# Quarter products inside three of the seven block products of Q and K

## The chip, the cores and the metric

The kernel runs on one core of one Trainium2 chip. The metric is the device time of one execution in microseconds (us). The core has five engines that run side by side and wait for each other by semaphores: TensorE (PE; its weight loads are shown as PEld), VectorE (DVE), ScalarE (ACT), GpSimd (POOL) and SyncE (SP), which issues the transfers between HBM and the on-chip memory SBUF. Matrix products land in a third memory, PSUM, which here is held as four tiles of two banks each.

## The reference

Two layers of self-attention run one after the other on a batch of 8 images with 512 channels and 1024 positions, in float32. Cut to what matters:

```python
xn  = groupnorm(x) * gamma + beta                 # 8 groups in layer 0, 32 in layer 1
qkv = einsum('oc,bcn->bon', qkv_w, xn) + qkv_b    # 512 -> 3 x 512 channels
q, k, v = split(qkv)                              # 8 heads of 64 channels
attn = softmax(einsum('bhdi,bhdj->bhij', q, k) / 8)
out  = einsum('bhij,bhdj->bhdi', attn, v)
x    = einsum('oc,bcn->bon', proj_w, out) + proj_b + x
```

## The kernel before

A *unit* is one image in one layer; there are 16, numbered 0 to 15, and units 0 to 7 are layer 0. The main loop over `u` does, for each unit: Q, then K, then V (`projections`), then the output projection of the unit before (`project(old, ...)`), then `attention` of this unit. While attention runs, the next unit's input is normalised. The results of layer 0 go to HBM as `mid`. Every engine takes its instructions in the order in which the program writes them, and waits are set automatically between them from the tiles that they read and write.

**Seven block products.** `blocks` makes a 512 x 512 by 512 x 1024 product as two-by-two blocks with seven block products in place of eight (a fast matrix multiplication of the Strassen kind). The left factors, from the weights, are mixed once per layer (`mix_weights`), the right ones, from the activations, once per unit (`mix_right`). They are numbered 1 to 7 and used in the order 1, 6, 2, 7, 5, 4, 3. Three PSUM tiles gather the sums: `bx` (`apair[0]`), `by` (`sbank[0]`) and `bz` (`apair[1]`); the fourth, `sbank[1]`, is not used in this stage. A sum that is wanted more than once is copied or added into SBUF as `p1`, `u2`, `u3`. ScalarE's `c11` and VectorE's `others` write the four blocks of the result. `done` is called after each block product; it counts them as `g` and runs small jobs that were left for that place (`rest`): for example `g` = 10 is after K's third block product.

In Q and K one block product is four matmuls of 128 x 128 weights by 512 columns; in V, where the roles are exchanged, it is eight with 256 columns.

**Buffers that matter here.** The pool `ppool` has four buffers of 4 KB per partition. In attention they hold the exponentials `p`, between attentions the `u3` of Q, K and V and the four residual tiles `x` that `load_res` fetches. The `mid` stores (line 411) read the residual tiles, so the exponentials of the next attention get those buffers only when the stores are done. `vpool` has one buffer, V of the unit. `tpool` holds the mixed right factors, with the tags `x1`, `x2`, `x4` for the unit's input and `o1`, `o2`, `o4` for the attention output.

**SyncE's queue.** All transfers are issued by SyncE in program order: in a unit first the residual, then the next input (`load_xn`), in unit 7 the weights of layer 1 (`load_weights(1)`, which GpSimd then mixes), then the output projection's stores, then the small transfers of attention.

Of the kernel before, what the change touches and what calls it, by code (L numbers as in the profile page):

```python
# [11 lines left out]
F32 = mybir.dt.float32  # L12
# [6 lines left out]
P = 128  # L19
# [13 lines left out]
def fast_path(ctx, tc, x, qkv_wT, proj_wT, vecs, groups, out, flag):  # L33
# [14 lines left out]
    nc = tc.nc  # L48
    B, C, N = x.shape
    CC = C // P  # L50
    D = C // HEADS
    NT = N // P
    FD = 512
    NH = N // FD
    H = P // 2
    FD2 = FD // 2
    BL = 32
    SCALE = 1.0 / math.sqrt(D)
    assert D == H and C == FD

    def pool(name, bufs, **kw):
# [6 lines left out]
    vpool = pool("vpool", 1)  # L68
    qkpool = pool("qkpool", CC)
    ppool = pool("ppool", 4)  # L70
    accpool = pool("accpool", 2)
    tpool = pool("tpool", 1)
# [6 lines left out]
    mids = pool("mids", 1, space=bass.MemoryType.DRAM)  # L79


    sbank = [ps.tile([P, 2, FD], F32, tag=f"s{i}", name=f"s{i}") for i in range(2)]
# [8 lines left out]
    half = const.tile([P, CC], F32, name="half")  # L91
    okay = const.tile([P, 2 * BL], F32, name="okay")
    asum = const.tile([P, 2 * B * CC], F32, name="asum")
    mid = [mids.tile([C, N], F32, tag=f"mid{b}", name=f"mid{b}") for b in range(B)]

    units = [(l, b) for l in range(2) for b in range(B)]
# [54 lines left out]
    def mix_right(name, low, high):  # L151


        b11, b12 = low[:, :, :FD], low[:, :, FD:]
        b21, b22 = high[:, :, :FD], high[:, :, FD:]
        t1, t2, t4 = (
            tpool.tile([P, 2, FD], F32, tag=f"{name[0]}{k}", name=f"{name}_t{k}")
            for k in (1, 2, 4)
        )
        sub = nc.vector.tensor_sub  # L160
        parts = (
            partial(sub, t1, b12, b11), partial(sub, t2, b22, t1),
            partial(sub, t4, b21, t2), partial(sub, b12, b22, b12),
        )
        return {1: b11, 2: b21, 3: b22, 4: t4, 5: t1, 6: t2, 7: b12}, parts

    def load_proj(l, tag):
        w = wpool.tile([P, CC, C], F32, tag=tag, name=f"wproj_{l}_{tag}")
# [99 lines left out]
    class Unit:  # L268
        pass

    def blocks(name, left, right, tokens, c11, others, done, u3_in):

        bx, by, bz = apair[0], sbank[0], apair[1]
        sums = []

        def products(bank, k, start, stop):
            a, b = left[k], right[k]
            for i in range(4 if tokens else 2):  # L280
                if tokens:
                    dst = bank[:, i // 2, (i % 2) * FD2 : (i % 2 + 1) * FD2]
                else:
                    dst = bank[:, i, :]
                for c in range(2):
                    at, moving = (b, a) if tokens else (a, b)

                    nc.tensor.matmul(  # L288
                        dst, at[:, c, ts(i, P)], moving[:, c, :],
                        start=start and c == 0 and not (tokens and i % 2),  # L290
                        stop=stop and c == 1, skip_group_check=True,
                    )

        def work(pool, tag, k):
            sums.append(pool.tile([P, 2, FD], F32, tag=tag, name=f"{k}_{name}"))
            return sums[-1]

        products(bx, 1, True, False)
        p1 = work(accpool, "acc", "p1")
        nc.scalar.copy(p1, bx)  # L300
        done(sums)
        products(by, 6, True, False)
        u2 = work(trpool, "tr", "u2")
        nc.vector.tensor_add(u2, by, p1)  # L304
        done(sums)
        products(bx, 2, False, True)
        c11(bx)
        done(sums)
        products(by, 7, False, False)
        u3 = work(*u3_in, "u3")  # L310
        nc.vector.tensor_add(u3, by, p1)
        done(sums)
        products(bz, 5, True, False)
        others(1, 1, bz, u3)
        done(sums)
        products(by, 4, False, True)
        others(1, 0, by, p1)
        done(sums)
        products(bz, 3, False, True)
        others(0, 1, bz, u2)  # L320
        done(sums)

    def projections(w, rest):


        u = w.u
        l, _ = units[u]
        w.last = {"q": [], "k": [], "v": []}
        g = 0

        def done(_):
            nonlocal g
            g += 1
            for part in rest.get(g, ()):
                part()

        for sel, bias in (("q", QB), ("k", KB)):
            tiles = [
                qkpool.tile([P, N], F32, tag=sel, name=f"{sel}_{u}_{pr}") for pr in range(CC)
            ]  # L340

            def c11(bank):
                for i in range(2):
                    w.last[sel].append(
                        nc.scalar.activation(
                            tiles[i][:, :FD], bank[:, i, :], AF.Identity,
                            bias=vec[:, l, bias, i : i + 1],
                        )
                    )

            def others(r, h, bank, more):
                for i in range(2):
                    pr = 2 * r + i
                    w.last[sel].append(
                        nc.vector.scalar_tensor_tensor(
                            tiles[pr][:, ts(h, FD)], bank[:, i, :], vec[:, l, bias, pr : pr + 1],
                            more[:, i, :], ALU.add, ALU.add,
                        )
                    )

            left = w.lefts["qk".index(sel)]
            blocks(f"{sel}_{u}", left, w.right, False, c11, others, done, (ppool, "p"))
            setattr(w, sel, tiles)

        w.v = vpool.tile([P, NT, C], F32, tag="v", name=f"v_{u}")

        def of_tokens(t):
            return t.rearrange("p a (b o) -> p (a b) o", b=2)

        def v11(bank):  # L370
            w.last["v"].append(nc.scalar.copy(w.v[:, : NT // 2, :FD2], of_tokens(bank)))

        def v_others(r, h, bank, more):
            w.last["v"].append(
                nc.vector.tensor_add(  # L375
                    w.v[:, ts(h, NT // 2), ts(r, FD2)], of_tokens(bank), of_tokens(more)
                )
            )

        blocks(f"v_{u}", w.lefts[2], w.right, True, v11, v_others, done, (ppool, "p"))  # L380
# [72 lines left out]
            )  # L453
            nc.sync.dma_start(dst[o * P : (o + 1) * P, ts(h, FD)], cols)

    def attention(w, at_step):


        u = w.u
# [39 lines left out]
        def products(s):  # L499
            p = state["p"][s]  # L500
            c, t = divmod(s, NT)
            pr, qh = divmod(c, NH)
            banks = abank[2 * (c % 2) : 2 * (c % 2) + 2]
            before = [state["exp"][s]]
            if t == 0:
                before += state["free"][c % 2]
            if s == 0:
                before += w.last["v"] + w.evac_before
            gate(*before)
            for r in range(2):  # L510
                rows = slice(r * H, (r + 1) * H)
                for j in range(2):
                    lo = pr * P + j * D
                    nc.tensor.matmul(  # L514
                        banks[r][j * H : (j + 1) * H, :],
                        w.v[rows, t, lo : lo + D],
                        p[rows, j, :],
                        start=(t == 0),
                        stop=(t == NT - 1),
                    )  # L520
# [14 lines left out]
        def evacuate(c):  # L535
            pr, qh = divmod(c, NH)
            banks = abank[2 * (c % 2) : 2 * (c % 2) + 2]
            tmp = tmppool.tile([P, FD], F32, tag="tmp", name=f"tmp_{u}_{c}")
            i0 = nc.scalar.copy(tmp, banks[0])  # L539
            i1 = nc.vector.tensor_add(w.ao[pr // 2][:, pr % 2, ts(qh, FD)], banks[1], tmp)  # L540
            state["free"][c % 2] = [i0, i1]
# [71 lines left out]
        for s in range(n_steps):  # L613
            c, t = divmod(s, NT)
            p = scores(s)
# [13 lines left out]
            summed(s, p)  # L629
            at_step(s, state)  # L630
        products(n_steps - 1)
        evacuate(n_chunks - 1)

        for h in range(NH):
# [6 lines left out]
            for h in range(NH):  # L641
                add_bias(CC - 1, h)

        w.right_o, mixing = mix_right(f"o_{u}", *w.ao)
        return {4: [lambda: reciprocals(CC - 1)], 10: [divide_last], 12: mixing[:2], 14: mixing[2:]}


    xn = load_xn(0)
# [2 lines left out]
    lefts, mixing_w = mix_weights(0, load_weights(0), nc.vector)  # L651
# [11 lines left out]
    old = None  # L663
    for u in range(2 * B):
        w = Unit()
        w.u, w.right, w.lefts = u, right, lefts
        w.evac_before = []
        for part in mixing[2:]:
            part()
        if u == B + 1:  # L670
            rest[16] = mixing_o
        projections(w, rest)
# [12 lines left out]
        if u == B - 1:  # L685
            lefts, mixing_w = mix_weights(1, load_weights(1), nc.gpsimd)
            for part in mixing_w:
                part()

        def stats_of(*which):  # L690
            for i in which if nxt is not None else ():
# [36 lines left out]
            elif c == 2 + CC and t in (2, 5):  # L728
                mixing[int(t == 5)]()

        rest = attention(w, at_step)
        old = w

    both = const.tile([P, 1], F32, name="both")
# [275 lines left out]
```

## Time and profile before

| | |
|---|---|
| time, median of 3 runs | 3342.32 us (3341.9 to 3342.86) |
| span in the profile | 3340.0 us |
| TensorE busy | 3315.5 us, 99% |
| VectorE busy | 2375.6 us, 71% |
| ScalarE busy | 1393.5 us, 42% |
| GpSimd busy | 48.1 us, 1% |
| mean granted TensorE clock | 0.999 |
| from HBM / to HBM | 110.26 MB / 34.08 MB |

Busy time is the time in which an engine had an instruction in execution; the profile's other parts give the chain of waits that ended last, groups of like instructions with the idle time before them, and the transfers. Times within the execution count from the start of the span. A unit takes some 207 us: Q, K, V and the output projection 24 us each, the rest attention.

### The profile page before, as it was taken

Reading aid. Unit: us, or ns where it says so; the run is one execution under the profiler, and the core shown is the slowest. Engines: PE = TensorE matmul, PEld = TensorE weight load, DVE = VectorE, ACT = ScalarE, POOL = GpSimd, SP = SyncE. Lnnn points to the kernel's source line nnn. Section 1 sums busy time; section 2 is a strip of 40 time slices with the busy share of each in tenths; the row PEclk is TensorE's granted clock in tenths of the full one; section 3 lists DMA queues with packets and bytes.
Section 4 is the critical chain, followed back from the end, with each engine's and each line's share of the span. In section 5 each row is a group of like instructions: output and inputs, shape, how many; then the busy total and the mean of one; then the engine's idle time right before and its main releaser. Section 6 shows DMA issues by size and latency. Waiting matters only on the chain.

```text
span 3340.0 us, 51079 instructions
## 1 busy us (share of the span) xinstructions
PE 3315.5 (99%) x21002; PEld 1645.3 (49%) x21002; DVE 2375.6 (71%) x2977; ACT 1393.5 (42%) x1549; POOL 48.1 (1%) x32
## 2 busy tenths in 40 slices
PE   8999999999999999999999999999999999999999
PEld 4445454454544545455554544545445454454533
DVE  4876948769486684867848678585785957859577
ACT  1542706336063360733617235172451724517144
POOL 0000000000000000002000000000000000000000
PEclk9999999999999999999999999999999999999999
DMA  2011010110101102012020111201111011110121
GB/s 78 33 39 58 21 64 27 39 58 22 70 27 33 58 21 76 21 33 96 21 85 25 33 58 28 76 15 33 64 33 64 15 37 60 33 63 15 39 71 47
DMA packets 66844, 149.27 MB, mean 45 GB/s; under 512 B 20784, under 2 KB 21040, under 8 KB 66608
## 3 DMA queue, kind: packets, MB, share of 16 engines
q1 hardware_dynamic: 66608, 145.95, 13.3%
q8 instruction: 169, 2.77, 0.4%
q14 instruction: 67, 0.55, 0.1%
HBM read 110.26 MB, written 34.08 MB: 43 GB/s over the span
## 4 chain that ended last, share of the span: by engine, by line
PE 98%; DVE 1%; issue 0%; DMA 0%; ACT 0%; POOL 0%; SPq 0%; DVEq 0%
PE a L514 26%; PE a L288 26%; PE s L486 25%; PE s L288 19%; PE a L486 1%; PE s L437 0%; PE a L437 0%; DMA xn<-x_dram 0%; DVE acc L533 0%; DVE x L422 0%; DVE stats L184 0%; PE a L196 0%; DVE tr L546 0%; DVE u_o L390 0%; POOL y L216 0%
## 5 line engine op out<-in xcount | busy, mean ns | idle before, releaser
L494 ACT ACTIVATE p<-s 128x1024 f32<-128x1024 f32 x976 | 997.2, 1023 | 816.7 <-PE s L486 761.7
L514 PE MATMUL a<-p,v 64*64 64x512 f32 x8192 | 1101.2, 589 | 0.1
L486 PE MATMUL s<-q,k 64*64 64x512 f32 x7808 | 1059.3, 590 | 1.4 <-DVE v L375 1.4
L533 DVE TENSOR_TENSOR acc<-acc,p 128x1024 f32<-128x1024 f32 x768 | 938.7, 1222 | 88.8 <-ACT p L494 41.4
L514 PEld LDWEIGHTS a<-p,v 64*64 64x64 f32 x8192 | 384.9, 131 | 494.4 <-ACT p L494 349.6
L486 PEld LDWEIGHTS s<-q,k 64*64 64x64 f32 x7808 | 385.8, 133 | 437.1 <-issue 434.6
L288 PE MATMUL a<-xn,w 128*128 128x512 f32 x512 | 234.4, 601 | 4.0 <-DVE xn L244 4.0
L531 DVE TENSOR_TENSOR acc<-p,p 128x1024 f32<-128x1024 f32 x128 | 153.7, 1201 | 12.9 <-ACT p L494 12.9
L288 PEld LDWEIGHTS a<-xn,w 128*128 128x128 f32 x512 | 96.9, 192 | 132.7 <-issue 128.1
L546 DVE STREAM_TRANSPOSE tr<-acc 128x1024 f32<-128x1024 f32 x128 | 158.0, 1234 | 0.0
L556 DVE TENSOR_REDUCE red<-tr 128x32 f32<-128x1024 f32 x128 | 153.9, 1202 | 0.6
L540 DVE TENSOR_TENSOR ao<-a,tmp 128x512 f32<-128x512 f32 x128 | 88.0, 687 | 69.9 <-ACT tmp L539 69.9
L300 ACT COPY p_k<-a 128x1024 f32<-128x1024 f32 x16 | 16.2, 1012 | 255.1 <-PE a L288 255.1
L300 ACT COPY p_o<-a 128x1024 f32<-128x1024 f32 x15 | 15.2, 1012 | 244.2 <-PE a L288 244.2
L288 PE MATMUL a<-w,xn 128*128 128x256 f32 x512 | 115.7, 379 | 0.0
L288 PE MATMUL s<-xn,w 128*128 128x512 f32 x256 | 115.2, 593 | 0.4 <-DVE u_q L304 0.4
L300 ACT COPY p_v<-a 128x1024 f32<-128x1024 f32 x16 | 16.2, 1012 | 237.3 <-PE a L288 221.4
L288 PE MATMUL s<-x_t,s2w 128*128 128x512 f32 x256 | 115.1, 592 | 0.0
L288 PE MATMUL a<-x_t,s1w 128*128 128x512 f32 x256 | 115.1, 592 | 0.0
L288 PE MATMUL s<-x_t,w 128*128 128x512 f32 x256 | 115.1, 592 | 0.0
L288 PE MATMUL a<-xn,s4w 128*128 128x512 f32 x256 | 115.1, 592 | 0.0
L288 PE MATMUL a<-ao,wproj_wproj 128*128 128x512 f32 x240 | 107.9, 592 | 0.0
(129 smaller groups left out, 2843.4 us busy)
## 6 DMA issues: line engine op xcount, KB each, us to landing
rb<-drec SPq DMA_DIRECT2D x128, 256.0 KB, 3.9
xn<-mid SPq DMA_DIRECT2D x36, 512.0 KB, 5.0
xn<-x_dram SPq DMA_DIRECT2D x32, 512.0 KB, 5.1
x<-x_dram SPq DMA_DIRECT2D x32, 512.0 KB, 4.6
mid<-x SPq DMA_DIRECT2D x64, 256.0 KB, 2.1
x<-mid SPq DMA_DIRECT2D x28, 512.0 KB, 4.6
out_dram<-x SPq DMA_DIRECT2D x56, 256.0 KB, 2.1
w<-qkv_wT_dram SPq DMA_DIRECT2D x6, 1024.0 KB, 11.2
```

The lines of the kernel that those rows point to most:

```text
L288: nc.tensor.matmul(dst, at[:, c, ts(i, P)], moving[:, c, :], start=start and c == 0 and not (tokens and i % 2), stop=stop and c == 1, skip ...
L300: nc.scalar.copy(p1, bx)
L486: nc.tensor.matmul(bank[e * H : (e + 1) * H, j, :], w.k[pr][j * H : (j + 1) * H, t * P + e * H : t * P + (e + 1) * H], w.q[pr][j * H : (j ...
L494: exp = nc.scalar.activation(p, bank, AF.Exp, scale=SCALE)
L514: nc.tensor.matmul(banks[r][j * H : (j + 1) * H, :], w.v[rows, t, lo : lo + D], p[rows, j, :], start=(t == 0), stop=(t == NT - 1),)
L531: nc.vector.tensor_add(acc, state["first"], p)
L533: nc.vector.tensor_add(acc, acc, p)
L540: i1 = nc.vector.tensor_add(w.ao[pr // 2][:, pr % 2, ts(qh, FD)], banks[1], tmp)
L546: nc.vector.transpose(tr, state["acc"].pop(c))
L556: nc.vector.tensor_reduce(red[:, :, qh, :], state["tr"].rearrange("p j (f i) -> p j f i", i=BL), AX.X, ALU.add)
```

## The change

In units 1 to 15, three of the seven block products of Q and of K, those numbered 2, 3 and 4 (`INNER`), are themselves made by the same seven-product scheme, with quarter products of one 128 x 128 weight block by 256 columns. Of eight such quarters seven remain. They come in the order 1, 2, 3, 6, 5, 4, 7.

For this the quarter products need mixed factors of their own:

- The right factors are made in each unit by GpSimd, four additions of 128 x 256 for each of the three block products (`mix_inner`), into three buffers of `ppool`. The `u3` of Q and K, which lay there, moves into the end of the V buffer.
- The left factors are made once per layer by GpSimd (`mix_inner_left`, in units 0 and 7: 24 additions of 128 x 128), written to HBM by six transfers, and read back at the end of every attention into the V buffer, two loads of 1152 numbers per partition (`load_inner_left`).

Parts of the quarter products that can't be summed in the block product's own bank are gathered in free PSUM banks (`one`, `two`) and copied by ScalarE to an SBUF tile `rest`, four copies of 128 x 256 for each block product. `one` is copied out between its uses and goes on accumulating. Later GpSimd adds the parts of `rest` together and adds them to the tiles of Q or K (`add_rest`, `rests`): two additions of 128 x 256 and two of 128 x 512 for each block product. Since `rest` lies in the `o` buffers of `tpool`, mixing the right factors of the attention output moves from K's blocks (`g` = 12 and 14) to V's (17, 19 and 20).

```diff
+    def mix_inner(u, right):
+        gp = nc.gpsimd
+        factors, parts = {}, []
+        for k in INNER:
+            b = right[k]
+            b11, b12 = b[:, 0, :FD2], b[:, 0, FD2:]
+            b21, b22 = b[:, 1, :FD2], b[:, 1, FD2:]
+            t = ppool.tile([P, 4, FD2], F32, tag="p", name=f"r{k}_{u}")
+            t1, t2, t3, t4 = (t[:, i, :] for i in range(4))
+            parts += [
+                partial(gp.tensor_sub, t1, b12, b11), partial(gp.tensor_sub, t2, b22, t1),
+                partial(gp.tensor_sub, t3, b22, b12), partial(gp.tensor_sub, t4, b21, t2),
+            ]
+            factors[k] = {1: b11, 2: b21, 3: b22, 4: t4, 5: t1, 6: t2, 7: t3}
+        return factors, parts
...
+    def mix_inner_left(l, lefts):
+        add, sub = nc.gpsimd.tensor_add, nc.gpsimd.tensor_sub
+        for n, k in enumerate(INNER):
+            t = tpool.tile([P, 2, FD], F32, tag=("o1", "o2", "o4")[n], name=f"l{k}_{l}")
...
+            for i in range(2):
...
+                add(s1, a21, a22)
+                sub(s2, s1, a11)
+                sub(a21, a11, a21)
+                sub(s4, a12, s2)
+                nc.sync.dma_start(inner_left[l][:, i, n], t[:, i])
+
+    def load_inner_left(u):
+        l, _ = units[u]
+        flat = vpool.tile([P, NT, C], F32, tag="v", name=f"il_{u}").rearrange("p t o -> p (t o)")
...
+            nc.sync.dma_start(part, inner_left[l][:, i])
...
+        def last_products(bank, k, one, two):
...
+            rest = tpool.tile([P, 2, FD], F32, tag=tag, name=f"m{k}_{name}")
...
+            product(1, one, True, False)
+            nc.scalar.copy(rest[:, 0, :FD2], one)
+            product(2, bank[:, 0, :FD2], False, True)
+            product(3, bank[:, 0, FD2:], False, True)
+            product(6, one, False, False)
+            nc.scalar.copy(rest[:, 0, FD2:], one)
+            product(5, two, True, True)
+            nc.scalar.copy(rest[:, 1, FD2:], two)
+            product(4, bank[:, 1, :FD2], False, True)
+            product(7, one, False, True)
+            nc.scalar.copy(rest[:, 1, :FD2], one)
+            return rest
+
+        def add_rest(r, h, rest):
+            if rest is not None:
+                add = nc.gpsimd.tensor_add
+                add(rest[:, 0, FD2:], rest[:, 0, FD2:], rest[:, 1, FD2:])
+                add(rest[:, 1, FD2:], rest[:, 1, :FD2], rest[:, 1, FD2:])
+                rests(r, h, rest)
...
-        products(bx, 2, False, True)
+        rest = last_products(bx, 2, sbank[1], bz)
         c11(bx)
+        add_rest(0, 0, rest)
...
-        products(by, 4, False, True)
+        rest = last_products(by, 4, bx, sbank[1])
         others(1, 0, by, p1)
+        add_rest(1, 0, rest)
         done(sums)
-        products(bz, 3, False, True)
+        rest = last_products(bz, 3, sbank[1], bx)
         others(0, 1, bz, u2)
+        add_rest(0, 1, rest)
         done(sums)
...
+            def rests(r, h, rest):
+                for i in range(2):
+                    cols = tiles[2 * r + i][:, ts(h, FD)]
+                    w.last[sel].append(nc.gpsimd.tensor_add(cols, cols, rest[:, i, :]))
...
         products(n_steps - 1)
+        at_end()
         evacuate(n_chunks - 1)
...
-        return {4: [lambda: reciprocals(CC - 1)], 10: [divide_last], 12: mixing[:2], 14: mixing[2:]}
...
+            17: [partial(mix, 0, 1)], 19: [partial(mix, 2)], 20: [partial(mix, 3)],
...
+        if u > 0:
+            w.made = old.made_next
+            w.inner, parts = mix_inner(u, right)
+            for part in parts:
+                part()
...
+        if u in (0, B - 1):
+            mix_inner_left(units[u + 1][0], lefts)
...
+        def at_end():
+            if u + 1 < 2 * B:
+                w.made_next = load_inner_left(u + 1)
```

More of the change, by code (lines that the diff above doesn't have):

```diff
@@ L58, in fast_path @@
     SCALE = 1.0 / math.sqrt(D)
+    INNER = (2, 3, 4)
     assert D == H and C == FD
@@ L93, in fast_path @@
     asum = const.tile([P, 2 * B * CC], F32, name="asum")
+    inner_left = [
+        mids.tile([P, 2, len(INNER), 3, P], F32, tag=f"il{l}", name=f"il{l}") for l in range(2)
+    ]
     mid = [mids.tile([C, N], F32, tag=f"mid{b}", name=f"mid{b}") for b in range(B)]
@@ L165, in mix_right @@
         return {1: b11, 2: b21, 3: b22, 4: t4, 5: t1, 6: t2, 7: b12}, parts
+    def mix_inner(u, right):
[10 more added lines that the diff above has]
+                partial(gp.tensor_sub, t3, b22, b12), partial(gp.tensor_sub, t4, b21, t2),
+            ]
+            factors[k] = {1: b11, 2: b21, 3: b22, 4: t4, 5: t1, 6: t2, 7: t3}
+        return factors, parts
@@ new lines, in inner_lefts @@
+    def inner_lefts(k, left, made):
+        a11, a12 = left[:, 0, :P], left[:, 1, :P]
+        a21, a22 = left[:, 0, P:], left[:, 1, P:]
+        s1, s2, s4 = (made[:, i, :] for i in range(3))
+        return {1: a11, 2: a12, 3: s4, 4: a22, 5: s1, 6: s2, 7: a21}
+    def mix_inner_left(l, lefts):
+        add, sub = nc.gpsimd.tensor_add, nc.gpsimd.tensor_sub
+        for n, k in enumerate(INNER):
+            t = tpool.tile([P, 2, FD], F32, tag=("o1", "o2", "o4")[n], name=f"l{k}_{l}")
+            t = t.rearrange("p a b -> p (a b)")[:, : 6 * P].rearrange("p (i s o) -> p i s o", i=2, s=3)
+            for i in range(2):
+                left = lefts[i][k]
+                a11, a12 = left[:, 0, :P], left[:, 1, :P]
+                a21, a22 = left[:, 0, P:], left[:, 1, P:]
+                s1, s2, s4 = (t[:, i, j, :] for j in range(3))
+                add(s1, a21, a22)
[3 more added lines that the diff above has]
+                nc.sync.dma_start(inner_left[l][:, i, n], t[:, i])
@@ new lines, in load_inner_left @@
+    def load_inner_left(u):
+        l, _ = units[u]
+        flat = vpool.tile([P, NT, C], F32, tag="v", name=f"il_{u}").rearrange("p t o -> p (t o)")
+        n = len(INNER) * 3 * P
+        made = []
+        for i in range(2):
+            part = flat[:, i * n : (i + 1) * n].rearrange("p (k s o) -> p k s o", s=3, o=P)
+            nc.sync.dma_start(part, inner_left[l][:, i])
+            made.append({k: part[:, j] for j, k in enumerate(INNER)})
+        return made, flat[:, NT * C - 2 * FD :].rearrange("p (a b) -> p a b", a=2)
@@ L269, in fast_path, with blocks @@
         pass
-    def blocks(name, left, right, tokens, c11, others, done, u3_in):
+    def blocks(name, left, right, tokens, c11, others, done, u3, inner=None, rests=None):
         bx, by, bz = apair[0], sbank[0], apair[1]
@@ L292, in products, with product @@
                     )
+        def last_products(bank, k, one, two):
+            if inner is None:
+                products(bank, k, False, True)
+                return None
+            left, right = inner[k]
+            one, two = one[:, 0, :FD2], two[:, 0, :FD2]
+            tag = ("o1", "o2", "o4")[INNER.index(k)]
+            rest = tpool.tile([P, 2, FD], F32, tag=tag, name=f"m{k}_{name}")
+            def product(j, dst, start, stop):
+                nc.tensor.matmul(
+                    dst, left[j], right[j], start=start, stop=stop, skip_group_check=True
+                )
+            product(1, one, True, False)
[16 more added lines that the diff above has]
+                rests(r, h, rest)
         def work(pool, tag, k):
@@ L305, in blocks @@
         done(sums)
-        products(bx, 2, False, True)
+        rest = last_products(bx, 2, sbank[1], bz)
         c11(bx)
+        add_rest(0, 0, rest)
         done(sums)
         products(by, 7, False, False)
-        u3 = work(*u3_in, "u3")
+        if isinstance(u3, tuple):
+            u3 = work(*u3, "u3")
+        else:
+            sums.append(u3)
         nc.vector.tensor_add(u3, by, p1)
@@ L359, in others @@
                     )
-            left = w.lefts["qk".index(sel)]
-            blocks(f"{sel}_{u}", left, w.right, False, c11, others, done, (ppool, "p"))
+            def rests(r, h, rest):
+                for i in range(2):
+                    cols = tiles[2 * r + i][:, ts(h, FD)]
+                    w.last[sel].append(nc.gpsimd.tensor_add(cols, cols, rest[:, i, :]))
+            i = "qk".index(sel)
+            left, inner, u3 = w.lefts[i], None, (ppool, "p")
+            if w.inner:
+                made, u3 = w.made
+                inner = {
+                    k: (inner_lefts(k, left[k], made[i][k]), w.inner[k]) for k in INNER
+                }
+            blocks(f"{sel}_{u}", left, w.right, False, c11, others, done, u3, inner, rests)
             setattr(w, sel, tiles)
@@ L454, in project_last, with attention @@
             nc.sync.dma_start(dst[o * P : (o + 1) * P, ts(h, FD)], cols)
-    def attention(w, at_step):
+    def attention(w, at_step, at_end):
         u = w.u
@@ L642, in divide_last, with mix @@
                 add_bias(CC - 1, h)
-        w.right_o, mixing = mix_right(f"o_{u}", *w.ao)
-        return {4: [lambda: reciprocals(CC - 1)], 10: [divide_last], 12: mixing[:2], 14: mixing[2:]}
+        mixing = []
+        def mix(*which):
+            if not mixing:
+                w.right_o, parts = mix_right(f"o_{u}", *w.ao)
+                mixing.extend(parts)
+            for i in which:
+                mixing[i]()
+        return {
+            4: [lambda: reciprocals(CC - 1)], 10: [divide_last],
+            17: [partial(mix, 0, 1)], 19: [partial(mix, 2)], 20: [partial(mix, 3)],
+        }
     xn = load_xn(0)
@@ L665, in fast_path @@
         w = Unit()
-        w.u, w.right, w.lefts = u, right, lefts
+        w.u, w.right, w.lefts, w.inner = u, right, lefts, None
         w.evac_before = []
@@ L729, in at_step @@
                 mixing[int(t == 5)]()
-        rest = attention(w, at_step)
+        def at_end():
+            if u + 1 < 2 * B:
+                w.made_next = load_inner_left(u + 1)
+        rest = attention(w, at_step, at_end)
         old = w
```

## The prediction

> **What bounds the kernel now.** I read the page from the top: busy times, then the chain that ended last, then the costliest groups.
>
> ```profile
> PE 3315.5 (99%) x21002; PEld 1645.3 (49%) x21002; DVE 2375.6 (71%) x2977; ACT 1393.5 (42%) x1549; POOL 48.1 (1%) x32
> ...
> PE 98%; DVE 1%; issue 0%; DMA 0%; ACT 0%; POOL 0%; SPq 0%; DVEq 0%
> ...
> L539 ACT COPY tmp<-a 128x512 f32<-128x512 f32 x128 | 74.3, 581 | 23.9 <-PE a L514 23.9
> ...
> L300 ACT COPY p_k<-a 128x1024 f32<-128x1024 f32 x16 | 16.2, 1012 | 255.1 <-PE a L288 255.1
> ...
> x<-x_dram SPq DMA_DIRECT2D x32, 512.0 KB, 4.6
> ```
>
> TensorE is busy 99% and is 98% of the chain, so only a shorter matrix stream or new TensorE idling can move the time. GpSimd (POOL) is almost unused. The last three rows are prices used below: a ScalarE copy of 512 and of 1024 columns out of PSUM, and a 512 KB load.
>
> The timeline gives the pace of the matrix stream; columns are start, length, engine, line, operation, operands. These are products of Q (512 columns) at the start of unit 5:
>
> ```profile
> 1035.20 3.60 PE L288 MATMUL s<-x_t,s2w 128*128 128x512 f32 x8
> ...
> 1038.63 3.60 PE L288 MATMUL a<-xn,w 128*128 128x512 f32 x8
> ...
> 1042.06 3.60 PE L288 MATMUL s<-xn,w 128*128 128x512 f32 x8
> ...
> 1042.26 1.26 ACT L345 ACTIVATE q<-a,vec 128x512 f32<-128x512 f32 x2 [5.86 <-PE a L288]
> ```
>
> A block product takes 1038.63 - 1035.20 = 3.43 us for 8 records (each written float32 matmul shows as two), so 0.429 us a record. ScalarE starts reading 0.20 us after the next block's first start. In V the records have 256 columns:
>
> ```profile
> 1514.01 3.62 PE L288 MATMUL a<-s4w,xn 128*128 128x256 f32 x16
> ...
> 1517.47 3.60 PE L288 MATMUL a<-ao,wproj_wproj 128*128 128x512 f32 x8
> ```
>
> 16 of them take 3.46 us, or 0.215 each: half the columns cost half the time.
>
> Last, the hand-over to attention in unit 7, where the change puts one-time work:
>
> ```profile
> 1528.42 1.27 POOL L688 TENSOR_TENSOR s1w<-w 128x512 f32<-128x512 f32 x1 [165.85 <-DMA w<-qkv_wT_dram]
> ...
> 1528.75 15.47 SPq L411 DMA_DIRECT2D mid<-x  x8
> ...
> 1541.59 1.95 PE L486 MATMUL s<-q,k 64*64 64x512 f32 x16
> ...
> 1543.05 1.94 ACT L494 ACTIVATE p<-s 128x1024 f32<-128x1024 f32 x2 [20.90 <-DMA mid<-x]
> ...
> 1543.97 1.27 POOL L688 TENSOR_TENSOR s4w<-w,s2w 128x512 f32<-128x512 f32 x1
> ...
> 1544.90 1.07 PE L514 MATMUL a<-p,v 64*64 64x512 f32 x8
> ```
>
> The first exponential waits for a `mid<-x` store, because its output `p` takes the buffer of a residual tile that must first be stored. Even now the stores end just in time.
>
> **What the Trainium skill says.** "GPSIMD Engine Reference", section 3.1, gives 4497 ns for a GpSimd two-input add of 2048 float32. The trace shows 1.27 us for 512, and section 1's SBUF interface shared with VectorE fits the 1.71 us seen when VectorE is busy. "Perfetto Trace Analysis", section "DMA Instruction — HWDGE (DVE, Sync)", says that the issuing sequencer itself waits for a transfer's semaphore and is free only afterwards: one waiting transfer holds all behind it. Here SyncE does wait inside its queue for the `mid<-x` producers. "TensorE: Matmul & The Clock Gate", section "What's actually happening", has the clock fall to half in idle windows; the first 8 matmuls, after an idle start, agree:
>
> ```profile
> 16.96 6.32 PE L288 MATMUL a<-xn,w 128*128 128x512 f32 x8 [3.95 <-DVE xn L244]
> ```
>
> Their successor starts at 23.12, so they took 6.16 us and not 3.43: 2.7 us lost.
>
> **The change part by part.**
>
> *Removed.* In units 1 to 15, three block products of Q and three of K become 7 quarter products each, of two 256-column records: 14 x 0.215 = 3.01 us for 3.43. Saved: 0.43 us, times 6 x 15 = 90, is 38.6 us, all on TensorE and so on the path.
>
> *Added waits in the quarter products.* `one` and `two` are copied out by ScalarE before they are used again. Two quarter products (0.86 us) always lie between a product's end and the reuse. In that time: 0.20 us until ScalarE starts; the copy of 256 columns, by the line through 581 and 1012 ns, 0.37; the release; the weight load, 0.19 us in the trace. The release is read from attention:
>
> ```profile
> 1009.48 1.02 ACT L494 ACTIVATE p<-s 128x1024 f32<-128x1024 f32 x1
> ...
> 1010.62 0.49 PEld L514 LDWEIGHTS a<-p,v 64*64 64x64 f32 x8 [0.37 <-ACT p L494]
> ```
>
> It is 0.12 us. The sum 0.20 + 0.37 + 0.12 + 0.19 = 0.88 is 0.02 over 0.86. There are 8 such waits in Q, 8 in K (two in each block, one more where the next block takes `two` over), so 240: 4.6 us. Bounds: 0 if the load needn't wait, 0.12 each (29 us) if the whole hand-over is exposed. Behind the waiting matmul all of TensorE is queued. I take the sum, since each term is from a row.
>
> *GpSimd.* No row has 256 or 128 columns. Between proportional (0.64, 0.32) and the 512-column price (1.27) I take the line through the trace's 1.27 us and the skill's 4.5: 0.73 and 0.46, an estimate. The right factors are 12 x 0.73 = 8.8 us per unit. Their buffers come free in turn as the last `p` tiles are added up: four adds from 1025.86 to 1031.05 hold p_58 to p_61, so product 2's factors are ready near 1033, and its blocks come at 1038.6 (unit 5). Product 4's follow the VectorE mix ending at 1038.8: ready near 1043, wanted near 1048. The corrections are 6 x (2 x 0.73 + 2 x 1.27) = 24 us per unit; the last of K ends some 6 us into V, and attention waits for it only 48 us after K. So 33 us of GpSimd lie beside TensorE at no cost, twice as slow included except for product 4's factors.
>
> *Factors from HBM.* Two loads of 576 KB per unit leave when V's buffer is free, at the last attention product. With 4.6 us for 512 KB the first lands near +5.5 us; the third quarter product asks for it after two blocks and two quarters, 7.7 us. Hidden by 2 us; the second is for K, 24 us on.
>
> *Moved.* Mixing the attention output's right factors goes from K to V. VectorE has room there (the windows give it 8.6 us busy in unit 5's 24 us of V), and the output projection begins later: nothing. The extra copies, 24 x 0.37 = 9 us per unit, find ScalarE mostly idle in Q and K: no cost beyond the waits. VectorE's evacuations are as before.
>
> *One-time factors.* In unit 0 nothing waits behind them. In unit 7, 24 GpSimd adds follow the weight mixing that ends at 1545.24, and their six HBM writes stand in SyncE's queue ahead of unit 6's `mid<-x` stores. GpSimd ends at 1545.2 + 24 x 0.46 = 1556.3. Then the last write's issue (0.35), five stores at 0.46, and 2.1 us to land (page's median) free the first `p` buffer at 1561.0 in place of 1543.05: 17.9 us in which TensorE can only run three scores ahead. With the half clock after it, 2.7: 20.6 us. Bounds: 24 x 0.32 gives 17; 0.6 an add gives 24.
>
> Sum: 3342.3 - 38.6 + 4.6 + 20.6 = 3328.9, say 3329 us.
>
> **The rivals.**
> 1. The hold-up in unit 7 doesn't reach TensorE (other buffers free first, or stores pass). Against it: the 20.90 us wait on `mid<-x` shows the dependency. Time: 3342.3 - 38.6 + 4.6 = 3308.
> 2. Buffer reuse becomes the bound: 0.12 us at each of 240 waits. For it: my margin is 20 ns and the 256-column copy isn't in the trace. Against: V keeps 0.215 us a record with a weight load for each. 3342.3 - 38.6 + 20.6 + 29 = 3353, slower than before.
> 3. The HBM factors or GpSimd's right factors come 2 us late in every unit: 15 x 2 = 30 us, 3359. For it: both loads start at once and share the DMA engines. Against: by the windows the four 512 KB loads of `xn` issued from 1104.20 are all in by 1112, 2 MB in some 7 us.
>
> **How the numbers follow.** Forecast 0.45, rivals 0.27, 0.17, 0.11. The border of 0.2% lies at 3335.6 and 3349.0. Faster: 0.41 of the forecast, all of rival 1, 0.02 of rival 3's short delays: 0.70. Same: 0.04 + 0.05 + 0.04 = 0.13. Slower: 0.12 + 0.05 = 0.17. The range 3305 to 3353 runs from rival 1 to rival 2 and leaves out most of rival 3 and the ends of both.
>
> **What would show it.** Right: inner blocks of about 3.05 us with pauses of tens of ns before the reused quarter; POOL near 520 us (15 x 33 + 48) with the idle before it not on the chain; one TensorE gap of some 18 us at the start of unit 7's attention, with ScalarE waiting for `mid<-x`; the other units about 2.3 us shorter (38.6 less 4.6, over 15). Wrong: TensorE waits of 0.1 us or more on the new copies, waits on the factor load in each unit, or no gap in unit 7.

## The result and the profile after

| | before | after |
|---|---|---|
| time, median of 4 runs | 3342.17 us (3341.9 to 3342.86) | 3348.67 us (3348.15 to 3349.08) |
| ratio after / before | | 1.0019 (95% interval 1.0002 to 1.0036) |
| span in the profile | 3340.0 us | 3346.6 us |
| TensorE busy | 3315.5 us | 3286.8 us |

The change makes the kernel slower by 6.5 us, or 0.2%, where 13 us less was forecast. The page of the changed kernel, first its busy times, its chain and the loads of the left factors:

```profile
PE 3286.8 (98%) x21542; PEld 1738.3 (52%) x21542; DVE 2411.0 (72%) x2977; ACT 1526.2 (46%) x1909; POOL 616.9 (18%) x620
...
PE 84%; DVE 11%; issue 3%; POOL 1%; DMA 1%; ACT 1%; SPq 0%; DVEq 0%; POOLq 0%; ACTq 0%
...
il<-il SPq DMA_DIRECT2D x30, 576.0 KB, 4.3
```

TensorE is busy 28.7 us less, so the shorter products are there, and yet the span is 6.6 us longer: TensorE idles now. VectorE, which had 1% of the chain, has 11%. TensorE's waits say for what (total us, times, longest):

```profile
PE s L348 <- DVE u_q L400: 18.0, 15, 2.7
PE a L627 <- ACT p L607: 17.4, 1, 17.4
```

One wait comes in each of the 15 changed units, for VectorE's `u2` of Q (shown as `u_q`); before, it came once, with 0.4 us. The other comes once in the run. This is the start of unit 5 in the timeline, VectorE and TensorE and one of GpSimd's right-factor additions:

```profile
1029.65 1.75 DVE L709 SCALAR_TENSOR_TENSOR ao<-ao,rb 128x1024 f32<-128x1024 f32 x1
...
1030.35 3.70 PE L348 MATMUL a<-xn,w 128*128 128x512 f32 x8
...
1031.33 3.40 DVE L646 TENSOR_TENSOR acc<-acc,p 128x1024 f32<-128x1024 f32 x2
...
1031.94 1.70 POOL L799 TENSOR_TENSOR r<-xn 128x256 f32<-128x256 f32 x1
...
1037.46 0.73 POOL L799 TENSOR_TENSOR r<-xn,r 128x256 f32<-128x256 f32 x1
...
1037.65 1.62 DVE L794 TENSOR_TENSOR x_t<-xn,x_t 128x1024 f32<-128x1024 f32 x1
...
1040.33 1.21 DVE L400 TENSOR_TENSOR u_q<-s,p_q 128x1024 f32<-128x1024 f32 x1
...
1041.60 3.70 PE L348 MATMUL s<-xn,w 128*128 128x512 f32 x8 [1.09 <-DVE u_q L400]
```

And the same VectorE instructions before the change, with TensorE's first product, in the timeline of unit 5 there:

```profile
1030.97 1.22 DVE L596 SCALAR_TENSOR_TENSOR ao<-ao,rb 128x1024 f32<-128x1024 f32 x1
...
1031.66 3.70 PE L288 MATMUL a<-xn,w 128*128 128x512 f32 x8
...
1032.11 2.55 DVE L533 TENSOR_TENSOR acc<-acc,p 128x1024 f32<-128x1024 f32 x2
...
1037.58 1.22 DVE L669 TENSOR_TENSOR x_t<-xn,x_t 128x1024 f32<-128x1024 f32 x1
...
1039.85 1.22 DVE L304 TENSOR_TENSOR u_q<-s,p_q 128x1024 f32<-128x1024 f32 x1
```

Before, `u2` started 1039.85 - 1031.66 = 8.19 us after the unit's first product; now it starts 1040.33 - 1030.35 = 9.98 us after it. The 1.79 us of delay are the division (1.75 for 1.22), two additions (3.40 for 2.55) and a mixing (1.62 for 1.22), which give 0.53 + 0.85 + 0.40 = 1.78. TensorE reuses the bank that `u2` reads, in the fourth block product, and since the third became shorter it asks for it earlier. An addition of GpSimd takes 1.70 us beside these instructions and 0.73 without them. That GpSimd's additions are what slows VectorE is so far only a coincidence in time; two of the experiments below test it.

From the starts in the trace, a unit's four products (Q, K, V and the output projection) took 96.47 us and now take 95.36. The six inner blocks take 3.02 us in place of 3.43, which saves 2.48; the wait takes about 1.26, and the weight load exposed after it 0.1. Unit 1 is worse than the others, at 98.69 us for 97.12: its wait is the longest, and four of the matmul records that follow it run at half pace, which takes 1.7 us more.

The single wait is at the start of unit 7's attention:

```profile
1542.40 9.17 SPq L212 DMA_DIRECT2D il<-l  x6
...
1550.78 0.46 POOL L211 TENSOR_TENSOR l<-w,l 128x128 f32<-128x128 f32 x1
...
1551.67 4.57 SPq L524 DMA_DIRECT2D mid<-x  x8
...
1556.71 1.94 ACT L607 ACTIVATE p<-s 128x1024 f32<-128x1024 f32 x2 [39.21 <-DMA mid<-x]
...
1557.88 1.98 PE L627 MATMUL a<-p,v 64*64 64x512 f32 x8 [17.41 <-ACT p L607]
```

SyncE issues the six factor writes, the last after GpSimd's last addition, which ends at 1551.24, and only then the first store of `mid`. It waits for GpSimd before these writes (32 us in all), and then for nothing more before the stores. The exponential waits for the stores, TensorE for the exponential; after the gap a group of eight matmuls takes 1.98 us for 1.07. That attention takes 130.57 us in place of 110.97.

### The profile page after: what moved, and what is told of

It reads as the page before. It is cut to its first block, busy times and chain, and to the rows that moved or that the text cites. A ratio compares the mean times of both kernels' runs of the same rounds, so it can differ in the third digit from the quotient of the medians.

```text
span 3346.6 us, 53654 instructions
## 1 busy us (share of the span) xinstructions
PE 3286.8 (98%) x21542; PEld 1738.3 (52%) x21542; DVE 2411.0 (72%) x2977; ACT 1526.2 (46%) x1909; POOL 616.9 (18%) x620
## 4 chain that ended last, share of the span: by engine, by line
PE 84%; DVE 11%; issue 3%; POOL 1%; DMA 1%; ACT 1%; SPq 0%; DVEq 0%; POOLq 0%; ACTq 0%
PE a L627 21%; PE s L599 21%; PE a L348 18%; PE s L348 15%; DVE acc L646 6%; PE a L366 4%; PE s L366 3%; DVE tr L659 1%; PE a L599 1%; DVE x_t L794 1%; ACT p L607 1%; DVE u_q L400 1%; DVE acc L644 1%; DVE xn L794 1%; DVE red L669 0%
## 5 line engine op out<-in xcount | busy, mean ns | idle before, releaser
L627 PE MATMUL a<-p,v 64*64 64x512 f32 x8192 | 1100.2, 590 | 17.5 <-ACT p L607 17.4
L646 DVE TENSOR_TENSOR acc<-acc,p 128x1024 f32<-128x1024 f32 x768 | 951.4, 1239 | 91.1 <-ACT p L607 42.7
L799 POOL TENSOR_TENSOR r<-xn 128x256 f32<-128x256 f32 x60 | 75.1, 1252 | 1197.9 <-DVE acc L646 1130.2
L275 POOL TENSOR_TENSOR y<-var,half 128x4 f32<-128x4 f32 x16 | 32.2, 2015 | 1004.8 <-DVE var L273 1004.8
L348 PE MATMUL a<-xn,w 128*128 128x512 f32 x272 | 126.8, 610 | 4.4 <-DVE xn L303 4.4
L466 POOL TENSOR_TENSOR k<-k,m_k 128x512 f32<-128x512 f32 x90 | 112.3, 1270 | 0.0
L466 POOL TENSOR_TENSOR q<-q,m_q 128x512 f32<-128x512 f32 x90 | 112.3, 1269 | 0.0
L348 PEld LDWEIGHTS a<-w,xn 128*128 128x128 f32 x512 | 97.3, 190 | 13.7 <-issue 0.5
```

Source lines behind the costliest of these rows:

```text
L348: nc.tensor.matmul(dst, at[:, c, ts(i, P)], moving[:, c, :], start=start and c == 0 and not (tokens and i % 2), stop=stop and c == 1, skip ...
L466: w.last[sel].append(nc.gpsimd.tensor_add(cols, cols, rest[:, i, :]))
L627: nc.tensor.matmul(banks[r][j * H : (j + 1) * H, :], w.v[rows, t, lo : lo + D], p[rows, j, :], start=(t == 0), stop=(t == NT - 1),)
L646: nc.vector.tensor_add(acc, acc, p)
```

## The experiments

**The left factors behind the output projection.** Theory: the place of the six writes in SyncE's queue makes the gap.

```diff
-        if u in (0, B - 1):
-            mix_inner_left(units[u + 1][0], lefts)
...
             project(old, lambda g: stats_of(*stats_after.get(g, ())))
...
+        if u in (0, B - 1):
+            mix_inner_left(units[u + 1][0], lefts)
```

> The mixing of the left factors for the quarter products and its six HBM writes are moved behind the output projection of unit 6, so that the mid stores stand ahead of them in SyncE's queue. If the queue caused the gap in unit 7: the 17.4 us TensorE wait there and the half clock after it are gone, unit 7's attention takes about 111 us in place of 130.6, and the time falls by about 19.6 us to 3329. Rival, the stores are late for another reason (GpSimd or the DMA engines are busy with the weights): the gap stays above 10 us and the time above 3338.

Measured: 3326.18 us, ratio to the kernel before, run on the same chip, 0.9958 (0.9943 to 0.9973). Unit 7's attention takes 111.2 us. In its timeline the stores start early, and the first exponential waits for its scores and no longer for a store:

```profile
1529.08 7.29 SPq L524 DMA_DIRECT2D mid<-x  x6
...
1535.23 1.94 ACT L607 ACTIVATE p<-s 128x1024 f32<-128x1024 f32 x2 [20.83 <-PE s L599]
...
1537.34 1.43 POOL L208 TENSOR_TENSOR l<-w 128x128 f32<-128x128 f32 x1
```

GpSimd mixes the left factors afterwards, beside attention. The edit moves the additions and their writes together; that the stores stood behind the writes is read from SyncE's queue above. With both moved the gap is gone: the queue order was its cause. The wait on `u_q` stayed at 18.0 us in all.

**No right factors.** Theory A blames GpSimd's additions for the late `u2`, rival B the shorter third block product alone.

```diff
-            t = ppool.tile([P, 4, FD2], F32, tag="p", name=f"r{k}_{u}")
...
-            factors[k] = {1: b11, 2: b21, 3: b22, 4: t4, 5: t1, 6: t2, 7: t3}
+            factors[k] = {1: b11, 2: b21, 3: b22, 4: b21, 5: b11, 6: b12, 7: b22}
```

> Leaves out GpSimd's 12 additions per unit for the right factors; the quarter products take unmixed blocks, so Q and K are not the reference's. Theory A, these additions slow VectorE's two-input instructions at the start of a unit and so u2 of Q comes late: the wait on u_q falls from 18.0 us in all to under 2, VectorE's additions there take 1.22 us again, and the time is near 3327. Rival B, the shortened block product 2 (0.41 us less) alone uses up the slack of u2: the wait stays above 10 us, time 3340 or more.

The kernel has a fast path, which all of this document is about, and a slow one that follows it when the softmax sums leave the range that the fast one accepts. With unmixed factors they do leave it, so the whole took 10779.61 us. That time says nothing on the change; the fast path is the first part of the trace, up to 3330 us. There TensorE's wait for `u_q` is left once, with 0.8 us, and the timeline of unit 5 shows VectorE at its old pace:

```profile
1020.73 1.22 DVE L703 SCALAR_TENSOR_TENSOR ao<-ao,rb 128x1024 f32<-128x1024 f32 x1
...
1021.43 3.70 PE L342 MATMUL a<-xn,w 128*128 128x512 f32 x8
...
1021.88 2.55 DVE L640 TENSOR_TENSOR acc<-acc,p 128x1024 f32<-128x1024 f32 x2
...
1029.62 1.22 DVE L394 TENSOR_TENSOR u_q<-s,p_q 128x1024 f32<-128x1024 f32 x1
...
1031.42 3.60 PE L342 MATMUL s<-xn,w 128*128 128x512 f32 x8
```

`u2` starts 8.19 us after the unit's first product, exactly as before the change. The four products of the unit take 94.00 us: 96.47 less 2.48 is 93.99, so the whole saving arrives. Rival B falls: the third block product is as short here, and `u2` is in time.

**The right factors alone.** The kernel before, with nothing but the 12 additions; none of the products changes.

```diff
+        if u > 0:
+            _, parts = mix_inner(u, right)
+            for part in parts:
+                part()
```

> The kernel before with nothing added but the 12 GpSimd additions per unit, whose results nobody reads. Theory A: VectorE is slowed here too, u2 of Q ends some 1.8 us later, 0.5 to 1.0 us after TensorE wants the bank, and the time rises by 10 to 18 us to 3352 to 3360. Rival B: the additions cost nothing, the time stays at 3342.

Measured, in one run: 3358.27 us beside 3341.38 for the kernel before, 17 us more. Unit 5 in its timeline:

```profile
1035.41 1.75 DVE L615 SCALAR_TENSOR_TENSOR ao<-ao,rb 128x1024 f32<-128x1024 f32 x1
...
1037.09 3.41 DVE L552 TENSOR_TENSOR acc<-acc,p 128x1024 f32<-128x1024 f32 x2
...
1043.42 1.73 DVE L688 TENSOR_TENSOR x_t<-xn,x_t 128x1024 f32<-128x1024 f32 x1
...
1047.47 3.70 PE L307 MATMUL s<-xn,w 128*128 128x512 f32 x8 [0.80 <-DVE u_q L323]
```

The same instructions are slowed by about the same amounts, and TensorE waits. The unit's products take 97.54 us, 1.07 more than before, and over the 15 units these stages take 17.2 us more, which is the whole difference. Nobody reads the results of these additions; that they run is enough.

**One mixing behind `u2`.** Of the VectorE work ahead of `u2`, the third mixing of the unit's right factors isn't wanted until the sixth block product.

```diff
-        for part in mixing[2:]:
-            part()
...
+            mixing[3]()
...
+            for part in parts[:8]:
+                part()
+            rest[2] = [mixing[2], *parts[8:]]
```

> The third mixing of the unit's right factors on VectorE (1.2 to 1.6 us) stands behind u2 of Q, and GpSimd's four additions for block product 4 behind it. Theory A and B both say that VectorE's chain ahead of u2 bounds: u2 ends 1.2 to 1.6 us earlier, the wait on u_q falls below 5 us in all, and the time falls by 16 to 20 us to about 3330. Rival C, the wait moves on to block product 4, whose factors now come late: a new TensorE wait of 1 us or more per unit there, time above 3340.

Measured: 3328.66 us, ratio 0.9962 (0.9947 to 0.9977). The wait on `u_q` is left once, 1.6 us, and no wait for block product 4's factors appears. The units' products take 94.22 us, 0.2 above those without right factors.

**No corrections.** GpSimd's other work, 24 of its 36 additions in a unit, is left out.

```diff
             if rest is not None:
-                add = nc.gpsimd.tensor_add
-                add(rest[:, 0, FD2:], rest[:, 0, FD2:], rest[:, 1, FD2:])
-                add(rest[:, 1, FD2:], rest[:, 1, :FD2], rest[:, 1, FD2:])
-                rests(r, h, rest)
+                pass
```

> Leaves out GpSimd's corrections of Q and K (24 additions per unit, 24 us), so Q and K are not the reference's; if its sums leave the range that the fast path accepts, a second, slow path follows it and only the first part of the trace is read. Theory A: these additions lie beside TensorE; the projection stages of a unit stay at 95.36 us and the gap in unit 7 at 17 us. Rival D, the corrections load the shared memory port too and cost as well: the stages fall by 0.3 us or more per unit, 5 us in all.

Measured: 3348.12 us in the one run, the time of the changed kernel. The products of units 4 and 5 take 95.35 and 95.36 us, the waits are 17.8 and 17.4 us. These additions, some 24 us per unit and the larger part of what the change gave GpSimd, cost nothing where they stand. They do slow VectorE: its addition of 32 x 64 named `one<-red,lt` takes 0.71 us beside them in unit 5 of the changed kernel and 0.20 here. But no wait of TensorE hangs on that. Rival D falls as to the time.

**Both repairs.** The first and the fourth edit together.

> Both repairs together, the left factors behind the output projection and the third mixing behind u2. If the two losses are independent, as the theory has it: 3348.7 less 22 less 20, about 3306 us, ratio about 0.989. If they were one and the same wait, it stays near 3326.

Measured: 3308.83 us, ratio 0.9901 (0.9884 to 0.9917). In parts of the time before, the two repairs alone took 0.0061 and 0.0057 off the changed kernel's 1.0019, and together 0.0118. The sum fits losses that are independent, and neither wait is in the trace as it was: the one of 17.4 us is gone, and the one for `u_q` is left once, with 1.6 us in unit 1.

**Another buffer for the first right factors.** Both repairs, and the tiles asked for in another order.

```diff
+        ts_ = {
+            k: ppool.tile([P, 4, FD2], F32, tag="p", name=f"r{k}_{u}") for k in (3, 4, 2)
+        }
...
-            t = ppool.tile([P, 4, FD2], F32, tag="p", name=f"r{k}_{u}")
+            t = ts_[k]
```

> As the run with both repairs, and block product 2's right factors take the buffer that comes free last of the three, so that GpSimd starts only when p_62 has been added up and not during the division and the additions before it. If the contention of GpSimd and VectorE is what is left: the projection stages fall from 94.22 to 94.0 us per unit and the time by about 3 us against the run with both repairs. If the factors now come too late for block product 2: a new TensorE wait at the third quarter product and more time.

Measured: 3309.28 us, ratio 0.9902. This tested nothing: GpSimd's first addition still starts 1.82 us before the unit's first product, and the division still takes 1.75 us. The order in which the tiles are asked for did not move it.

**A wait for GpSimd.** What that edit was meant to do, by a wait: the first of the 12 additions waits for VectorE's last addition of the attention before.

```diff
-                nc.vector.tensor_add(acc, acc, p)
+                w.last_sum = nc.vector.tensor_add(acc, acc, p)
...
+                if n == 0:
+                    tc.add_manual_dep(
+                        getattr(i, "ins", i), name_of(old.last_sum), DEP, reason="after the sums"
+                    )
```

> As the run with both repairs, and GpSimd's first right-factor addition of a unit also waits for VectorE's last addition of the attention before, so that none of the 12 runs beside the division and the two additions there. Theory A: those VectorE instructions take 1.22 us each again and end some 1.4 us earlier, the 0.1 us exposed weight load at the fourth block product goes, the projection stages fall from 94.22 to 94.0 us per unit, and the time falls by about 3 us to 3306. Rival: the factors of block product 2 now come late, a new TensorE wait before its fourth quarter product appears, and the time rises.

Measured: 3306.47 us, ratio 0.9894 (0.9877 to 0.9910), the fastest version here, 35 us under the kernel before on its chip (3341.88). The step from both repairs is smaller than the intervals of the two ratios, so the trace has to show it. Unit 5 in its timeline:

```profile
1020.52 1.22 DVE L709 SCALAR_TENSOR_TENSOR ao<-ao,rb 128x1024 f32<-128x1024 f32 x1
...
1021.67 2.55 DVE L646 TENSOR_TENSOR acc<-acc,p 128x1024 f32<-128x1024 f32 x2
...
1024.35 0.73 POOL L801 TENSOR_TENSOR r<-xn 128x256 f32<-128x256 f32 x1 [85.67 <-DVE acc L646]
...
1027.14 1.22 DVE L797 TENSOR_TENSOR xn<-xn 128x1024 f32<-128x1024 f32 x1
...
1027.22 1.72 POOL L801 TENSOR_TENSOR r<-xn 128x256 f32<-128x256 f32 x1
...
1031.21 3.60 PE L348 MATMUL s<-xn,w 128*128 128x512 f32 x8
```

VectorE is back at 1.22 us an instruction, GpSimd, which starts 5 us later, still delivers in time, and the fourth block product follows the third without a pause. The units' products take 94.08 us, 0.14 us less in a usual unit. Unit 1, where the last wait for `u_q` is gone, takes 1.5 us less. Over the 15 units that is 3.1 us, beside 3.3 us between the two profiled spans and 2.4 between the medians.

## Why the prediction was wrong

- *Saved: 38.6 us.* Right in mechanism, and near in size. The forecast's own 3.46 us for 16 records is 0.216 us each and not 0.215, so an inner block takes 3.02 us and saves 0.41 in place of 0.43. That is 2.48 us a unit and 37.2 in 15 units; without the right-factor additions this saving arrives whole.
- *The waits in the quarter products: 4.6 us.* They cost nothing. A copy of 256 columns takes 0.372 us, as the line through two longer ones said, but the sum of 0.88 us was a little too large: the hand-over fits into the two quarter products. In all 90 inner blocks each record starts 0.215 to 0.216 us after the one before, the pace of V's records, also where `one` or `two` is used again. Rival 2 fell. In unit 5 the second and the last of these quarter products reuse `one`:

```profile
1038.18 0.59 PE L366 MATMUL a<-xn,il 128*128 128x256 f32 x2
1038.62 0.59 PE L366 MATMUL s<-r,il 128*128 128x256 f32 x2
1039.05 0.59 PE L366 MATMUL a<-r,il 128*128 128x256 f32 x2
1039.48 0.59 PE L366 MATMUL a<-r,w 128*128 128x256 f32 x2
1039.91 0.59 PE L366 MATMUL s<-r,w 128*128 128x256 f32 x2
```

- *The factors from HBM: hidden.* Right: a load lands in 4.3 us (median), and TensorE waits for none. Rival 3 fell for these loads.
- *Unit 7: 20.6 us.* Right, by the path that was named. The wait is 17.4 us, and the attention with the slow clock 19.6 us longer; a transfer's wait in the issuing queue holds all behind it, as the Trainium skill has it in "Perfetto Trace Analysis", section "DMA Instruction — HWDGE (DVE, Sync)". Rival 1 fell.
- *GpSimd: "33 us of GpSimd lie beside TensorE at no cost, twice as slow included".* This is the step that failed. The prices were good (0.73, 0.46 and 1.27 us alone, as taken), and the question of whether GpSimd's own results come in time was answered rightly. ("POOL near 520 us" was a wrong sum: 15 x 33 + 48 is 543, and the page has 616.9: the 48 one-time additions, 22 us, were left out, and the right factors take 13.4 us a unit in place of 8.8.) What was not asked is what GpSimd does to its neighbour. The forecast quoted the SBUF interface that GpSimd shares with VectorE (the Trainium skill, "GPSIMD Engine Reference", section 1) and used it only to make GpSimd slower. It also makes VectorE slower: 1.78 us before `u2` of Q, where VectorE had under 1 us to spare. "VectorE's evacuations are as before" holds for how long they take (1.21 us for `u2`), and not for when: `u2` comes 1.79 us later. The cost is 1.26 + 0.1 us in a usual unit, more in unit 1, some 23 us in all, against nothing in the forecast: together with the 19.6 of unit 7 more than the 37.2 saved.

The sum as measured: 37.2 saved; 19.6 and some 0.3 lost in unit 7; of the rest, the usual units keep 1.11 us each, and unit 1, with its wait of 2.7 us and the half pace after it, loses 1.6. 14 x 1.11 - 1.6 - 19.9 = -6.0, beside the 6.5 us of the times.

## What to carry to other kernels

Work given to an idle engine is free only if both questions have an answer: does it finish in time, and which instructions of other engines run beside it on a shared port? Ask the second first where the neighbour's queue ends in something that the bounding engine reuses soon, and look for slack there in the trace of before, not in the neighbour's average load. And when one-time work is put into a program, look what is queued behind its transfers: the place in the program order can cost more than the work.

## What the runs showed of the hardware

- GpSimd and VectorE didn't merely slow each other; the durations fit instructions taking turns. A GpSimd addition of 256 columns takes 0.73 us alone and 1.5 to 1.8 beside VectorE's additions of 1.22 us, and VectorE's instruction that follows takes 1.6 to 1.75. In the last run the first to start kept its pace: VectorE's mixing at 1027.14 takes its 1.22 us, and GpSimd's addition, started 0.08 us later, takes 1.72. The clearest case is a small VectorE addition that starts just after one of GpSimd's corrections, in unit 5 of the last run. In the kernel before it takes 0.20 us; here it lasts until 0.08 us after GpSimd's addition ends. That they take turns is read from such durations and was not tested by an experiment of its own:

```profile
1036.39 1.26 POOL L466 TENSOR_TENSOR q<-q,m_q 128x512 f32<-128x512 f32 x1
...
1036.44 1.29 DVE L689 TENSOR_TENSOR two<-lt 32x64 f32<-32x64 f32 x1
```

- Of the VectorE instructions that ran beside these additions in unit 5, only those with two SBUF operands were slowed. Beside the same additions its transpose (1.23 us), its reduction (1.22) and its additions with one operand in PSUM (1.21) kept their times.
- After the gap of 17.4 us TensorE's matmuls ran at half pace for the first two groups of eight (granted clock 0.50 from 1558 to 1561 us), which with a third somewhat slow one makes the 2.2 us by which the attention is longer than the gap. A wait of 2.7 us was followed by half pace in one run and not in another. In unit 1 of the changed kernel the records after it took 0.85 us for 0.43 (granted clock 0.53 from 217.4 to 221); in the run with the left factors behind the output projection the same wait was followed by full pace. What decides between the two was not tested.
